# First columns of two matrices and second tokens loaded first; layer a's last step with rows in front of scores; the last rows and router pieces placed among later expert blocks

## The chip, the cores and the metric

The kernel runs on one core of one Trainium2 chip. The core has five engines with queues of their own: TensorE (PE in the profile, its weight loads PEld), VectorE (DVE), ScalarE (ACT), GpSimd (POOL) and SyncE (SP), which here only issues DMAs. Engines wait for each other by semaphores. The metric is the device time of one execution in microseconds (us); lower is better.

## The reference

Eight batches of 512 tokens with 256 features, in float32, go through four layers, each with a residual:

```
x = x + attention_a(layernorm(x))   # 16 heads of 64, causal, a linear bias by distance, out-projection with bias
x = x + experts(layernorm(x))       # RMS norm, router, the best 2 of 8 experts per token, gated two-layer MLP
x = x + attention_b(layernorm(x))   # 8 heads of 128, causal, rotary positions
x = x + experts(layernorm(x))       # the same expert weights again
```

Attention is `softmax(q k^T + bias) v` for each head, and the expert layer is

```
vals, idx = top_k(flat @ gate_w.T + gate_b, 2);  wts = softmax(vals)
t1 = einsum('td,efd->tef', flat, mlp1_w) + mlp1_b
y  = einsum('tei,edi->ted', swiglu(t1), mlp2_w) + mlp2_b
out = sum(y[idx] * wts)
```

## The kernel before

The four layers are one long program. `layer` emits an attention layer, `Experts.run` the expert layer behind it.

**Order of the instructions.** Only TensorE is scheduled by hand (`manual_schedule`, L120): it executes in the order in which the code emits. The other engines are ordered by the framework's planner, which takes the ready instruction that was emitted earliest; a DMA issue on SP counts as one. Once built, each engine's order is fixed, and an instruction that waits holds up all behind it on its engine.

**Attention.** A layer has 64 steps (b, g): batch b, head group g, two heads of layer a or one of layer b. A step (`step`, L503) of layer a emits the scores of the current group in three PSUM banks, then turns the probabilities of the group before (`turn`, 20 transposes in all), between them the q and k projections of the next group and the "extra" pieces due at this place, and at the end `average` of the group before. `scores` sends each bank through DVE (bias and row maximum, L407) and ACT (exponential with sums, L417); the rows are then divided by their sums, the longest by DVE and the other three by POOL (L434), and for the very last group of a layer all by DVE. `turn` copies the turned rows out by ACT, one bank of six by DVE (L457 to L459).

**Extras.** `layer` files every other piece under a key (b, g, k): the values, the out-projection, the norm of the next batch ((b, 5, 1), then applied and turned at (b, 6)), the router of the previous batch. What would fall behind the last batch is returned as a list: the last turns, the last average, two out-projections of the last half, and six router pieces of the last batch.

**Experts.** Tokens are gathered by expert into 71 blocks of 128 rows. `run` (L1049) is a pipeline over iterations n: it gathers block n + 4, turns the activations of block n - 5, turns the rows of block n (`turn_rows`), does the first matrix of block n - 2 (`first`) and the second matrix of block n - 6 (`second`), then the pieces that `aside` holds for n. `flush` (L1195) places the returned list and the second stage's six sorting pieces at iteration numbers.

`turn_rows` transposes a gathered row block and lets ACT copy it back: for the blocks below AHEAD (L86) in place, into the gather tile `g` (tag "qk", four blocks a tile, two tiles), for the others into the tile `turned`, which has the tag "O" (one buffer) and so takes the place of the attention's output O once the last out-projection has read it.

**Start.** `layers` issues on SP the tokens of batch 0 (two of four pieces on ACT's queue), then whole matrices: wq and wk (1 MB each, two rows of 4 KB per partition), alibi, the output bias, wv, wo, the router's constants, and the expert weights `we` in 16 pieces (6 MB together), then sin (L152 to L175). Batch b + 1's tokens are fetched by a piece at (b, 1, 1), into one of three "x" buffers (L1220). `fold_norm` lets POOL multiply the expert weights by the norm's weights (L243, 16 times).

Of the kernel before, what the change touches and what calls it, by code (L numbers as in the profile page):

```python
# [37 lines left out]
F32 = mybir.dt.float32  # L38
# [8 lines left out]
P = 128  # L47
NB, T, D = 8, 512, 256
NT = T // P
NC = D // P  # L50
INNER = 1024
# [31 lines left out]
LEAD = 4  # L83
ROWS = 4
DEPTH = 6
AHEAD = 3  # L86

W_COLS = NC * 2 * FI + FI // P * D
B_COLS = 2 * FI + D
# [4 lines left out]
def layers(  # L94
# [24 lines left out]
    nc = tc.nc  # L119
# [4 lines left out]
    wpool = ctx.enter_context(tc.tile_pool(name="wpool", bufs=1))  # L124
# [7 lines left out]
    def load(pool, shape, src, name, tag=None):  # L132
        t = pool.tile(shape, F32, tag=tag or name, name=name)
        nc.sync.dma_start(out=t, in_=src)
        return t

    def by_rows(w):
        return w.rearrange("(c p) n -> p c n", p=P)

    def by_tokens(x):  # L140
        return x.rearrange("(t p) d -> p t d", p=P)

    def load_x(src, name):
        return load(xpool, [P, NT, D], by_tokens(src), name, "x")

    X = {0: xpool.tile([P, NT, D], F32, tag="x", name="x0")}
    for t in range(NT):
        (nc.sync, nc.scalar)[t % 2].dma_start(
            out=X[0][:, t, :], in_=x_in[0][t * P : (t + 1) * P, :]
        )  # L150
    mask_sb = cos_sb = None
    wq = load(wpool, [P, NC, INNER], by_rows(a_qkv[:, 0:INNER]), "wq_a", "wq")  # L152
    wk = load(wpool, [P, NC, INNER], by_rows(a_qkv[:, INNER : 2 * INNER]), "wk_a", "wk")
    alibi_sb = load(const, [P, T], alibi, "alibi", "bias")
    bout_sb = load(const, [P, D], a_bout.partition_broadcast(P), "bout", "cos")
    wv = load(wpool, [P, NC, INNER], by_rows(a_qkv[:, 2 * INNER : 3 * INNER]), "wv_a", "wv")
    wo = load(wpool, [P, INNER // P, D], by_rows(a_out), "wo_a", "wo")
# [1 line left out]
    gatew_sb = load(const, [P, NC, NE], by_rows(gatew), "gatew")  # L159
    gateb_sb = load(const, [P, NE], gateb.partition_broadcast(P), "gateb")  # L160
    rank_sb = load(const, [P, NT, NE], rank, "rank")
    we_sb = const.tile([P, NE * W_COLS], F32, tag="we", name="we")
    be_sb = const.tile([P, NE * B_COLS], F32, tag="be", name="be")
    for e in range(NE):
# [3 lines left out]
            out=we_sb[:, o:mid].rearrange("p (c f) -> p c f", c=NC),  # L168
            in_=w1[:, e, :].rearrange("(c p) f -> p c f", p=P),
        )  # L170
        nc.sync.dma_start(
            out=we_sb[:, mid : o + W_COLS].rearrange("p (c d) -> p c d", c=FI // P),
            in_=w2[:, e, :].rearrange("(c p) d -> p c d", p=P),
# [106 lines left out]
    class Attention:  # L280
# [155 lines left out]
        def turn(self, b, g, i, n):  # L436

            key = f"{self.kind}_{b}_{g}_{i}"
            S = self.S[b, g][i][0]
            if n == 0:  # L440
                self.PT[b, g, i] = work.tile([P, PACKED], F32, tag="PT", name=f"PT_{key}")
            bank = P_BANKS[n]
            base = P_OFF[bank[0]]
            tp = ps.tile([P, T], F32, tag="ps", bufs=8, name=f"tp_{key}_{n}")
            width = 0
            for jt in bank:
                for it in range(jt, NT):
                    o = P_OFF[jt] - base + (it - jt) * P
                    nc.tensor.transpose(  # L449
                        tp[:, o : o + P],  # L450
                        S[:, S_OFF[it] + jt * P : S_OFF[it] + (jt + 1) * P],
                        ident,
                    )
                    width += P
            pt = self.PT[b, g, i][:, base : base + width]
            if n == 0 and i == 1:
                nc.vector.tensor_copy(pt, tp[:, 0:width])  # L457
            else:
                nc.scalar.copy(pt, tp[:, 0:width])  # L459
# [43 lines left out]
        def step(self, last, cur, after, extra):  # L503

            there = set(self.qk)

            def scores(n):
                if cur:
                    self.scores(*cur, n)

            def turn(i, *banks):
                if last:
                    for n in banks:
                        self.turn(*last, i, n)

            def project(j):
                if after and after not in there:
                    self.project(*after, j)

            if self.kind == "a":  # L520
                scores(0)
                scores(1)
                scores(2)
                turn(0, 0, 1, 2)
                project(0)
                extra(1)
                turn(1, 0, 1, 2)
                project(1)
                extra(2)
            else:  # L530
                scores(0)
                project(0)
                turn(0, 0)
                scores(1)
                project(1)
                turn(0, 1, 2)
                scores(2)
                extra(1)
                extra(2)
            if last:  # L540
                self.average(*last)


    class Experts:
# [401 lines left out]
        def turn_rows(self, i, j):  # L946
# [7 lines left out]

            if m < AHEAD:
                h = g
            else:
                if m == AHEAD:
                    self.turned = work.tile([P, HALF * T // D, D], F32, tag="O", bufs=1, name=f"hT_{self.kind}")
# [234 lines left out]

    def flush(left, exp):  # L1195

        turns = (0, 2, 2, 2, 3, 5, 8, 10, 12, 14)
        aside = {}
        for n, piece in zip(turns, left, strict=True):
            aside.setdefault(n, []).append(piece)  # L1200
        for n, piece in zip((16, 18, 20, 22, 25, 28), exp.sorting(1), strict=True):
            aside[n] = [piece]
        return aside

# [2 lines left out]
    def fetch_a(b):  # L1207
        X[b] = load_x(x_in[b], f"x{b}")
# [8 lines left out]
    att_a.project(0, 0, 0)  # L1217
    att_a.project(0, 0, 1)
    more = [((0, 3, 1), spread_biases), ((1, 0, 1), fold_norm)]
    more += [((b, 1, 1), lambda b=b: fetch_a(b + 1)) for b in range(NB - 1)]  # L1220
    aside = flush(layer(att_a, exp_a, more), exp_a)
    aside.setdefault(6, []).append(weights_b)
    aside[done] = [lambda: exp_a.fetch(0)]
# [13 lines left out]
    more = []  # L1237
    for b in range(NB - 1):
        more.append(((b, 0, 1), lambda b=b: exp_a.fetch(b + 1)))
        for t in range(NT):  # L1240
            more.append(((b, t, 1), lambda b=b, t=t: exp_a.collect(b + 1, (t,), "tmp", both_queues)))
            more.append(((b, t + 1, 1), lambda b=b, t=t: exp_a.add(b + 1, (t,))))
    aside = flush(layer(att_b, exp_b, more), exp_b)

    def store(b, tiles, engine):
# [11 lines left out]
    for k, (b, tt) in enumerate(halves):  # L1257
        n = done + 3 * k // 2
        tag = ("xT", "PT")[k % 2] if k not in (8, 9) else "qk"
# [5 lines left out]
    end = TOTAL + DEPTH  # L1265
# [76 lines left out]
```

## Time and profile before

| | us |
|---|---|
| median of 3 runs | 2254.11 (2252.29 to 2255.5) |
| the profiled execution | 2239.6 |
| its span, first to last instruction | 2237.8 |

The profile is of one execution, by the hardware's own records; times in the views are us from the start of the span. TensorE's granted clock is 0.993 of full speed over the span. The costliest places of TensorE, by its rows: the expert matrices L982 257.8 us, the transposes L449 of layer a 166.2 us, the scores of layer b 169.7 us and of layer a 155.5 us, the averages of layer a 156.0 us. A timeline row gives start, duration, engine, line, operation, tiles, count, and in brackets how long the engine was idle before it and what it waited for. Some matmuls are drawn as overlapping, since their ends are modelled; the distance of their starts is the better measure.

The three places that the change touches lie in the span as follows: the start at 0 to 60 us, the end of layer a and the first expert blocks at 915 to 1020, the end of layer b and its expert blocks at 1970 to 2070.

| window, us | PE busy | DVE | ACT | POOL | PE clock | GB/s by DMA |
|---|---|---|---|---|---|---|
| 0 to 20 | 15.91 | 8.58 | 5.93 | 7.60 | 1.00 | 291 |
| 20 to 40 | 18.02 | 8.79 | 9.46 | 18.32 | 1.00 | 357 |
| 40 to 60 | 17.82 | 12.00 | 10.70 | 7.36 | 0.91 | 45 |

### The profile page before, as it was taken

The page shows a single profiled execution, that of the slowest core. Times are in us where ns is not written, and L with a number is a line of the kernel's source. Part 1 is how long each engine was busy: PE and PEld are TensorE (multiplying, and loading weights), DVE is VectorE, ACT ScalarE, POOL GpSimd, SP SyncE. Part 2 cuts the span into 40 slices and gives each one's busy share as a digit, 9 for nine tenths or more (in the row PEclk, how much of TensorE's full clock was granted, in tenths as well). Part 3 has the DMA queues.
Part 4 walks back from the last instruction along what each step waited for, and adds up shares of the span by engine and source line. Part 5 has one row for each costly group of instructions (what it writes and reads, how often), then busy time and mean ns, then how long its engine had stood idle before and what let it go on. Part 6 is the DMA issues. An engine that isn't in the chain of part 4 may idle for free.

```text
span 2237.8 us, 33567 instructions
## 1 busy us (share of the span) xinstructions
PE 2190.3 (98%) x10513; PEld 1429.2 (64%) x10513; DVE 1586.9 (71%) x4817; ACT 961.6 (43%) x2784; POOL 967.1 (43%) x1337
## 2 busy tenths in 40 slices
PE   8999999999999999999999999999999999999995
PEld 5666666666666666656666666666666666665663
DVE  4566666666666687687787676777777678968768
ACT  4555555555555555323324334434444433333331
POOL 5443434243433333266654343333434343356662
PEclk9999999999999999999999999999999999999997
DMA  7100000000000000232220010100101010042237
GB/s 248 39 15 15 6 24 1 30 1 29 1 29 1 29 6 29 99 106 84 90 76 29 10 39 10 39 29 19 48 6 43 6 34 1 19 139 78 85 101 252
DMA packets 78382, 108.80 MB, mean 49 GB/s; under 512 B 9568, under 2 KB 64000, under 8 KB 78208
## 3 DMA queue, kind: packets, MB, share of 16 engines
q1 hardware_dynamic: 62656, 67.58, 9.4%
q0 software_dynamic: 13632, 37.24, 5.4%
q8 instruction: 87, 1.43, 0.3%
q10 hardware_dynamic: 1920, 1.84, 0.3%
q14 instruction: 87, 0.71, 0.1%
HBM read 67.02 MB, written 39.60 MB: 48 GB/s over the span
## 4 chain that ended last, share of the span: by engine, by line
PE 88%; DVE 7%; issue 2%; ACT 1%; POOL 1%; SPq 1%; DMA 1%; DVEq 0%; ACTq 0%; POOLq 0%
PE pp_b L337 10%; PE hp_f L982 9%; PE pp_a L337 9%; PE op_a L476 6%; PE sp_b L395 6%; PE sp_a L395 6%; PE tp_a L449 6%; PE op_b L476 6%; PE yp_a L494 5%; PE yp_b L494 5%; PE vp_a L318 4%; PE y_f L1021 4%; PE vp_b L318 4%; PE tp_b L449 3%; PE gtp_f L953 1%
## 5 line engine op out<-in xcount | busy, mean ns | idle before, releaser
L417 ACT ACTIVATE S_a<-S_a,nm_a 128x512 f32<-128x512 f32 (+3 forms) x512 | 280.1, 548 | 313.7 <-DVE nm_a L407 309.9
L350 POOL TENSOR_TENSOR qk_b<-qk_b,rot_b 128x512 f32<-128x512 f32 x128 | 163.0, 1274 | 453.1 <-DVE qk_b L349 427.7
L376 POOL TENSOR_SCALAR ali_a<-alibi 128x512 f32<-128x512 f32 x128 | 79.3, 620 | 454.9 <-DVE nm_a L407 443.1
L982 PE MATMUL hp_f<-we,hT_f 128*128 x544 | 257.8, 596 | 4.3 <-DVE u_f L993 2.9
L417 ACT ACTIVATE S_b<-S_b,nm_b 128x512 f32<-128x512 f32 (+3 forms) x256 | 142.9, 559 | 241.1 <-DVE nm_b L407 233.4
L407 DVE CUSTOM_DVE_ANT_0 S_a<-sp_a,ali_a 128x512 f32<-128x512 f32 (+3 forms) x512 | 215.9, 487 | 30.7 <-PE sp_a L395 30.7
L434 POOL TENSOR_SCALAR S_a<-S_a,sum_a 128x384 f32<-128x384 f32 x378 | 203.1, 554 | 34.6 <-DVE sum_a L428 25.0
L1033 POOL DMA_INDIRECT y_f<-y_f,row_f x142 | 143.4, 1010 | 114.1 <-DVE y_f L1032 59.2
L407 DVE CUSTOM_DVE_ANT_0 S_b<-sp_b,mask 128x512 f32<-128x512 f32 (+3 forms) x256 | 119.4, 485 | 77.1 <-PE sp_b L395 76.7
L395 PE MATMUL sp_b<-qk_b 128*128 128x512 f32 (+3 forms) x512 | 169.7, 434 | 2.6 <-POOL qk_b L350 2.5
L449 PE MATMUL tp_a<-ident,S_a 128*128 128x128 f32 x1280 | 166.2, 276 | 5.4 <-DVE O_a L484 3.3
L939 POOL DMA_INDIRECT g_f<-h_all_f,token_f x142 | 144.4, 1017 | 59.4 <-issue 39.6
L449 PEld LDWEIGHTS tp_a<-ident,S_a 128*128 128x128 f32 x1280 | 141.3, 142 | 36.8 <-issue 21.3
L994 ACT ACTIVATE u_f<-u_f 128x256 f32<-128x256 f32 x142 | 59.2, 417 | 238.0 <-DVE u_f L993 179.5
L476 PE MATMUL op_a<-PT_a,V_a 128*64 128x384 f32 (+3 forms) x1024 | 156.0, 442 | 3.3 <-ACT S_a L417 2.2
L1021 PEld LDWEIGHTS y_f<-we,aT_f 128*128 128x128 f32 x568 | 108.8, 193 | 77.1 <-issue 59.6
L395 PE MATMUL sp_a<-qk_a 64*128 64x512 f32 (+3 forms) x1024 | 155.5, 443 | 0.9 <-DVE qk_a L354 0.9
L1021 PE MATMUL y_f<-we,aT_f 128*128 x568 | 148.6, 385 | 3.8 <-ACT aT_f L1012 3.7
L459 ACT COPY PT_a<-tp_a 128x512 f32<-128x512 f32 (+1 forms) x320 | 139.1, 496 | 29.4 <-PE tp_a L449 27.6
L476 PE MATMUL op_b<-PT_b,V_b 128*128 128x512 f32 (+3 forms) x512 | 148.7, 433 | 0.0
L993 DVE TENSOR_TENSOR u_f<-hp_f,be 128x512 f32<-128x512 f32 x142 | 98.2, 691 | 59.5 <-PE hp_f L982 20.5
L982 PEld LDWEIGHTS hp_f<-we,hT_f 128*128 128x128 f32 x544 | 92.7, 190 | 73.1 <-issue 66.3
(205 smaller groups left out, 4454.8 us busy)
## 6 DMA issues: line engine op xcount, KB each, us to landing
h_all_f<-hn_f SPq DMA_DIRECT2D x64, 128.0 KB
xm_f<-x_mid_f SPq DMA_DIRECT2D x16, 512.0 KB
yg_f<-y_f SPq DMA_DIRECT2D x32, 256.0 KB
yg_f<-y_f SPq DMA_DIRECT2D x56, 128.0 KB
we<-w_dram SPq DMA_DIRECT2D x8, 512.0 KB
x_mid_f<-x SPq DMA_DIRECT2D x8, 512.0 KB
x_mid_f<-xm_f SPq DMA_DIRECT2D x8, 512.0 KB
x<-x_in_dram SPq DMA_DIRECT2D x7, 512.0 KB
```

Source lines behind the costliest of these rows:

```text
L318: nc.tensor.matmul(vp[:, k, :], lhsT=self.xT[b][:, c, t * P : (t + 1) * P], rhs=wv[:, c, q * 2 * P : (q + 1) * 2 * P], start=(c == 0), sto ...
L337: nc.tensor.matmul(pp, lhsT=w[:, c, g * P : (g + 1) * P], rhs=self.xT[b][:, c, :], start=(c == 0), stop=(c == NC - 1),)
L350: nc.gpsimd.tensor_tensor(qk[:, j, :], qk[:, j, :], rot, ALU.add)
L395: nc.tensor.matmul(sp[i][:, at[it] : at[it] + w], lhsT=qk[r, 0, it * P : (it + 1) * P], rhs=qk[r, 1, 0:w], start=True, stop=True,)
L407: nc.vector.tensor_tensor_reduce(out=s, in0=sp[i][:, at[it] : at[it] + w], in1=add[i][:, T - w : T], scale=scale, scalar=float(np.finfo(np ...
L417: nc.scalar.activation(s, s, AF.Exp, bias=nm[:, it : it + 1], scale=-1.0, accum_out=sums[:, it : it + 1],)
L434: eng.tensor_scalar(s, s, sums[:, it : it + 1], 1.0, ALU.mult, ALU.mult)
L449: nc.tensor.transpose(tp[:, o : o + P], S[:, S_OFF[it] + jt * P : S_OFF[it] + (jt + 1) * P], ident,)
L476: nc.tensor.matmul(op[i * cols : (i + 1) * cols, jt * P : T], lhsT=v[:, jt, c0 : c0 + cols], rhs=PT[i][:, P_OFF[jt] : P_OFF[jt] + T - jt * P],
L494: nc.tensor.matmul(yp[:, 0:D], lhsT=o[:, c, t * P : (t + 1) * P], rhs=wo[:, half * HALF + c, :], start=(c == 0), stop=(c == HALF - 1),)
L982: nc.tensor.matmul(hp, lhsT=h[:, c * P : (c + 1) * P], rhs=we_sb[:, bass.DynSlice(wat + c * 2 * FI, 2 * FI)], start=(c == 0), stop=(c == N ...
L1021: nc.tensor.matmul(yp, lhsT=aT[:, c * P : (c + 1) * P], rhs=we_sb[:, bass.DynSlice(wat + NC * 2 * FI + c * D, D)], start=(c == 0), stop=(c ...
```

## The change

The diff has four parts. At the start, wq and wk are each loaded in two pieces: the first 256 of 1024 columns of both, then alibi, then the other 768 columns of both. Batch 1's tokens are loaded in front of the expert weights instead of by the piece at (0, 1, 1). The last step of layer a emits the turns of the group before in front of the scores, without projections (there is no next group). `flush`, for both layers, puts the list's pieces two iterations later (the last, the count, three), and the sorting pieces one to two later; AHEAD goes from 3 to 5, so that five blocks of rows are kept in place and O's buffer is taken over later.

```diff
-AHEAD = 3
+AHEAD = 5
...
-    wq = load(wpool, [P, NC, INNER], by_rows(a_qkv[:, 0:INNER]), "wq_a", "wq")
-    wk = load(wpool, [P, NC, INNER], by_rows(a_qkv[:, INNER : 2 * INNER]), "wk_a", "wk")
+
+    wq, wk = (wpool.tile([P, NC, INNER], F32, tag=tag, name=f"{tag}_a") for tag in ("wq", "wk"))
+
+    def load_qk(first, end):
+        for k, w in enumerate((wq, wk)):
+            nc.sync.dma_start(
+                out=w[:, :, first:end],
+                in_=by_rows(a_qkv[:, k * INNER + first : k * INNER + end]),
+            )
+
+    load_qk(0, 2 * P)
     alibi_sb = load(const, [P, T], alibi, "alibi", "bias")
+    load_qk(2 * P, INNER)
...
     rank_sb = load(const, [P, NT, NE], rank, "rank")
+    X[1] = load_x(x_in[1], "x1")
...
-            if self.kind == "a":
+            if self.kind == "a" and not after:
+
+                turn(0, 0, 1, 2)
+                turn(1, 0, 1, 2)
+                for n in range(3):
+                    scores(n)
+                extra(1)
+                extra(2)
+            elif self.kind == "a":
...
-        turns = (0, 2, 2, 2, 3, 5, 8, 10, 12, 14)
+        turns = (2, 4, 4, 4, 5, 7, 10, 12, 14, 17)
...
-        for n, piece in zip((16, 18, 20, 22, 25, 28), exp.sorting(1), strict=True):
+        for n, piece in zip((18, 20, 22, 24, 26, 29), exp.sorting(1), strict=True):
...
-    more += [((b, 1, 1), lambda b=b: fetch_a(b + 1)) for b in range(NB - 1)]
+    more += [((b, 1, 1), lambda b=b: fetch_a(b + 1)) for b in range(1, NB - 1)]
```

## The prediction

> **What bounds the kernel.** I read the busy row and the chain of waits first, then TensorE's list of waits, then the timelines of the three places that the change touches.
>
> ```profile
> PE 2190.3 (98%) x10513; PEld 1429.2 (64%) x10513; DVE 1586.9 (71%) x4817; ACT 961.6 (43%) x2784; POOL 967.1 (43%) x1337
> PE 88%; DVE 7%; issue 2%; ACT 1%; POOL 1%; SPq 1%; DMA 1%; DVEq 0%; ACTq 0%; POOLq 0%
> ```
>
> TensorE (PE) is busy for 2190 of 2238 us and is 88% of the chain that ended last; most of VectorE's (DVE) 7% is the closing adds after the last matmul, at 2219 to 2234. The change removes no matmul, so it can win only PE's gaps before that tail, and what follows a gap. The gaps at its three places:
>
> ```profile
> PE tp_a L449 <- DVE O_a L484: 3.3, 2, 2.6
> PE op_a L476 <- ACT S_a L417: 2.2, 1, 2.2
> PE pp_a L337 <- DMA wk_a<-a_qkv_dram: 0.5, 1, 0.5
> PE tp_b L449 <- issue: 0.8, 1, 0.8
> PE yp_b L494 <- ACT O_b L486: 0.7, 1, 0.7
> ```
>
> Each line: waiter, releaser, us in total, times, longest. The first two cost more than they show, as the timelines (start, us, what, idle before) tell:
>
> ```profile
> 39.63 0.75 DVE L253 BATCH_NORM_STATS2 st_a<-x 128x6 f32<-128x256 f32 x2 [5.30 <-DMA x<-x_in_dram]
> 41.30 0.66 DVE L484 COPY O_a<-op_a 128x512 f32<-128x512 f32 x1
> ```
>
> ```profile
> 42.01 1.04 PE L449 MATMUL tp_a<-ident,S_a 128*128 128x128 f32 x6 [2.56 <-DVE O_a L484]
> 43.23 3.26 PE L337 MATMUL pp_a<-xT_a,wq_a 128*128 128x512 f32 x4 [0.17 <-DVE nm_a L407]
> 46.28 2.35 PE L318 MATMUL vp_a<-wv_a,xT_a 128*128 128x256 f32 x8
> 49.56 1.88 PE L337 MATMUL pp_a<-xT_a,wk_a 128*128 128x512 f32 x4
> ```
>
> DVE stands still 5.30 us for batch 1's tokens; the copy of O queues behind the statistics, and PE loses 2.56 us. Then four projection matmuls take 3.26 us instead of 1.88.
>
> ```profile
> 922.24 2.40 PE L449 MATMUL tp_a<-ident,S_a 128*128 128x128 f32 x20
> 926.88 1.07 PE L476 MATMUL op_a<-PT_a,V_a 128*64 128x512 f32 x2 [2.23 <-ACT S_a L417]
> 928.28 3.82 PE L476 MATMUL op_a<-PT_a,V_a 128*64 128x512 f32 x14 [0.34 <-issue]
> ```
>
> ```profile
> 928.00:932.00 4.00, 3.71 (x14) 1.67 (x14) 1.42 (x5) 0.86 (x2) 0.00 (x0) 0.59 0.13 37
> ```
>
> In layer a's last step the average waits while ScalarE (ACT) does the eight exponentials of step (7,7), which stand in front of its copies of the turned rows. In the last row (times by windows) the granted clock is 0.59.
>
> **The first gap's true price: a rule against a row.** The Trainium skill (TensorE: Matmul & The Clock Gate, Part 1) says that PE falls to half clock after an idle window of about 3.4 us, and its closing table allows gaps to about 3 us. By that rule, gaps of 2.56 and 2.23 us cost only themselves. The trace differs: in half-microsecond windows the clock is 0.50 from 44.0 to 46.5, and the pair of groups at 43.23 and 46.28 takes 1.38 + 0.46 = 1.8 us more than elsewhere (1.88 and 1.89); the 14 matmuls at 928.28 take 3.82 against about 2.05, 1.75 more. Yet a 2.23 us gap at 1886 leaves the clock at 1.00. So a gap of this size may double its price; here both did. By the rule the two waits are worth 2.7 + 2.6 us, by the rows 4.5 and 4.3; I take the rows.
>
> **Part 1, first columns first.** The k projection starts at 11.69, behind wk's load; q's ran from 9.20, when its weights' load had waited for xT too. The q and k columns needed first are 0.25 MB each, together half of wq, which had landed whole at 9.2. So they are there by then, and k can follow q at once, at 9.20 + 4 x 0.43 = 10.9: **0.8 us** earlier to the first scores. The columns behind (g = 2) are needed only at 28.9; wv is not late, since its bytes in front are the same. SyncE's queue (SP) gets two more issues, about 0.45 us each by its rows; at 7.21 to 13.4 it is held[...] anyway (gatew's issue takes 6.15), so between 0 and 0.9 us for what is behind. Here a rule speaks against the change: the skill (DMA: Bandwidth & Descriptors, section Bandwidth) wants transfers of 1 MiB and more, and its fit of 2.0 us plus bytes at 436 GB/s would make two extra pieces, run alone, an estimated 4 us dearer. The row: at 20 to 40 us pieces of 256 and 512 KB from this same queue move 357 GB/s, since they overlap. I charge nothing.
>
> **Part 2, batch 1's tokens in front of the expert weights.** They land where the first expert weights land now (20.85; equal bytes in front) plus up to 0.9: about 21.5, instead of 39.6. The 5.30 us stall at 34.3 goes: 2.56 + 0.17 + 1.8 = **4.5 us**. What is late next:
> - The 0.5 MB delays each expert weight by 0.5 / 0.36 = 1.4 us. GpSimd (POOL) scales those weights (16 x 0.69 us) in the gaps of its normalising:
>
> ```profile
> 25.75 0.69 POOL L243 TENSOR_SCALAR we<-we,normw 128x512 f32<-128x512 f32 x1
> 26.42 2.76 POOL L434 TENSOR_SCALAR S_a<-S_a,sum_a 128x384 f32<-128x384 f32 x6
> ```
>
> PE's transposes wait for the second row (27.41, idle 0.99). If POOL keeps this order, they start 1.4 us later, and a gap of 0.99 + 0.8 + 1.4 = 3.2 us would bring the half clock, 1.7 more: -3.1 in all. If fewer scalings stand in front, up to +0.8 stays.
> - All engines but PE are ordered by the framework's planner. It placed the statistics 5.3 us too early. If it does so again, after the first group's score reductions (end 19.1, then a gap of 1.4 for ACT), DVE stalls until 21.5, plus 2 us of statistics; the k copy at 22.37 then ends near 24.8, scores of group 1 start at 25.2 instead of 23.99, and the transposes at about 27.8: -0.4, since the wait for POOL swallows the rest.
>
> Between +0.8 and -3.1 I take -0.6, near the second bullet. Start: 4.5 - 0.6 = **3.9 us** (1.4 to 5.3).
>
> **Part 3, last step of layer a, pieces two blocks later.** Both orders have done the same work when iteration 4's matmuls end (block 2's first layer), now at 949.93. New order from 919.88: 20 transposes 2.36, to 922.2 (their rows, POOL's last S at 914.8, are ready; ACT is free to copy); scores 2.36, to 924.6; average 2.31, to 926.9, no wait, its copies being done near 923; three row turns 0.66, to 927.6. Then the **new wait**: block 0's matmul needs ACT's copy of its row, and ACT's exponentials (921.89 to 926.26) now run 2.36 later, to 928.6; copy 0.37 and the hand-over: 929.05, PE idle 1.5. Block 0 1.72, to 930.8. The last turns: DVE's normalised rows, now ready at 927.6 and 929.4, come at 929.9 and 931.8, in time; 20 transposes, to 933.1. Blocks 1 and 2 with their turns 2 x 1.94, average 2.31, projection 7.1: 946.4. Gain **3.5 us**. Bounds: the copy slips between exponentials (4.8); the copy is planned still later and the half clock returns (0.5).
>
> AHEAD = 5 keeps five rows in place, because the O buffer is freed only at iteration 4; then block 3 reads the first gather tile until about 948.4, and gather 8, which refills it, stands on POOL until then. Behind it POOL has the last batch's norm chain (now 947.46 to 952.5, no earlier in the new order) and further gathers. Row 8 is turned near 954.6; a gather at 949 lands well before. If POOL runs the whole norm chain first, it is some 1.2 us late: that is inside the bound. The sorting pieces move along and end at iteration 29 instead of 28; the second stage's first gather is at 37.
>
> **Part 4, the same delays in layer b** (its step order is unchanged). Average ends at 1976.34; the third gather leaves POOL at 1975.88, and its data burst ends near 1977.3, so row 2 costs some 0.6 us of idle; block 0 to 1979.4, last turns 1.10 (ready at 1977.8), blocks 1 and 2 3.9, average 2.16, projection 7.0 with 0.1 for ACT's copy (now 0.69 behind a table load): 1993.7 against 1994.91. **1.0 us**, bounds 0 and 1.5 (the two idles).
>
> **Sum.** 3.9 + 3.5 + 1.0 = 8.4 us. The profiled execution took 2239.6 (span 2237.8 and 1.8 around it) and would take 2231.2. The median shown is 2254.1, 14.5 above the profiled one; the same loss off it gives **2245.7**.
>
> **Rivals.**
> 1. *The start gives all back* (0.17): POOL keeps its order, the gap of 3.2 us and the half clock come, and the statistics stall DVE as well: 4.5 - 4.5 = 0, leaving 4.5: 2249.6. For it: POOL is 18.3 of 20 us busy from 20 to 40. Against: it has to be misplanned twice.
> 2. *Planning noise takes the ends* (0.13): ACT's row copies are put late in both layers, layer a gains 0.5, b nothing; with 3.9: 2249.7. For: DVE and ACT show such misorders (PE waits 1.0 at 966). Against: ACT is idle 8.4 us before 946.
> 3. *Slower* (0.20): the planner puts batch 1's statistics in front of DVE's **first k copy** (now 13.71). It decides there: DVE then stands until the tokens land, at 21.5, or near 25 if SP's queue is held for the small pieces as it is for gatew; with 2 us of statistics and the copy, the first scores start at 24.8 to 28.3 instead of 14.55: -10.2 to -13.7, half clock -1.7; the old stall's 4.5 and POOL's two waits, 1.2, come back: -6.2 to -9.7 for the start, and with the 4.5 of parts 3 and 4 a loss of 1.7 to 5.2: 2255.8 to 2259.3, say 2258.5. For: the planner expected these tokens 5 us too early. Against: at an equal error it expects them near 16, when that copy is past.
>
> Forecast: 0.50.
>
> **Range and chances.** The bounds add to 1.9 and 11.3; with the spread of runs, 1.6 either way, 2241 to 2254; I reach half a us further at both ends; rival 3 lies above and is left out. What can be told from no change is 0.2%, 4.5 us. Faster: 0.50 x 0.95, and half of rivals 1 and 2: 0.62. Slower: half of rival 3, 0.10; same: the rest, 0.28.
>
> **What would show it.** Right: no DMA wait before the statistics of batch 1, no half clock near 44 or 930; k's projection at 10.9; iteration 4 of layer a's experts done near 949.93 - 3.9 - 3.5 = 942.5. Wrong: a DMA wait on DVE before 20, POOL's first S later than 27, or PE idle over 2 us ahead of block 0. A norm chain ahead of gather 8, with PE waiting at row 8, would break part 3.

## The result, and the profile after

The changed kernel is slower by about a quarter of a per cent: median 2257.20 us of 20 runs (2252.84 to 2261.01) against 2250.92 (2243.05 to 2255.50) for 20 runs of the kernel before beside it, ratio 1.0027 with a 95% interval of 1.0019 to 1.0035. The forecast was 2245.7, which is 8.4 us under the 2254.1 that it counted from, with a range of 2241 to 2254; the change moved the time 6.3 us the other way. The profiled execution took 2257.87 us, span 2256.1, mean granted clock 0.990.

One caution first. The profiled execution of the kernel before, 2239.6 us, lies 11.3 us under the median of its 20 runs and under the fastest of them; that of the changed kernel lies at its median. The two traces stand 18.3 us apart where the medians stand 6.3; so what only these two traces show is not yet a loss of the change. The record does not say that they are of one chip; profiles of both kernels from one chip are used below.

The busy row and the chain's row of the page after:

```profile
PE 2195.6 (97%) x10513; PEld 1431.4 (63%) x10513; DVE 1587.7 (70%) x4817; ACT 960.7 (43%) x2784; POOL 959.9 (43%) x1337
PE 87%; DVE 8%; issue 2%; ACT 1%; DMA 1%; POOL 1%; DVEq 0%; SPq 0%; another core or an unknown queue 0%; POOLq 0%; ACTq 0%
```

TensorE still bounds it. Its list of waits (waiter, releaser: us in total, times, longest; hp_f and y_f are an expert block's first and second matrix, u_f and aT_f what VectorE and ScalarE make between them):

```profile
PE hp_f L1001 <- DVE u_f L1012: 7.7, 7, 2.2
PE y_f L1040 <- ACT aT_f L1031: 5.3, 5, 2.3
PE xtp_a L286 <- DVE xn_a L273: 4.3, 1, 4.3
PE gtp_f L972 <- DMA g_f<-h_all_f,token_f: 4.0, 3, 1.6
...
PE inv_f L900 <- DVE col_f L885: 1.7, 2, 0.9
```

Of the two waits that the prediction set out to remove, op_a for S_a is gone, and tp_a for O_a is down from 3.3 us in two waits to one of 0.7, the one that is not at the start. Two waits are new, gathered rows (gtp_f) and the sorting's tables (inv_f), and that of the first transposes of all (xtp_a) has grown from 0.3 us to 4.3.

**The start.** TensorE's timeline from 5 to 22 us:

```profile
10.09 2.23 PE L286 MATMUL xtp_a<-ident,xn_a 128*128 128x128 f32 x8 [4.28 <-DVE xn_a L273]
12.90 3.78 PE L348 MATMUL pp_a<-xT_a,wq_a 128*128 128x512 f32 x4 [0.57 <-DVE xT_a L317]
16.47 2.74 PE L348 MATMUL pp_a<-xT_a,wk_a 128*128 128x512 f32 x4
20.09 2.21 PE L406 MATMUL sp_a<-qk_a 64*128 64x512 f32 x14 [0.88 <-DVE qk_a L365]
```

and GpSimd's, in the same stretch:

```profile
5.37 0.20 POOL L267 TENSOR_SCALAR rs_a<-mv_a 128x4 f32<-128x4 f32 x1 [3.18 <-DVE mv_a L265]
7.45 0.61 POOL L387 TENSOR_SCALAR ali_a<-alibi 128x512 f32<-128x512 f32 x1 [1.88 <-DMA alibi<-alibi_dram]
8.14 1.04 POOL L268 TENSOR_TENSOR rs_a<-rs_a,mhalf 128x4 f32<-128x4 f32 x1
```

Alibi is now loaded behind 0.5 MB of weights instead of 2 MB, and the planner puts its scaling **between the two instructions of the first norm's root** (a scaling at L267 and a power at L268). GpSimd stands 1.88 us for alibi's DMA, the power ends near 9.2 instead of 6.45, VectorE's first normalised rows and TensorE's first transposes come 3 us late, and behind TensorE's gap of 4.28 us the projections run at half clock: 3.78 us for four matmuls instead of 1.95. The first scores come at 20.09 instead of 14.55. Batch 1's statistics then find their tokens there (VectorE's timeline, no wait in brackets):

```profile
22.45 0.75 DVE L264 BATCH_NORM_STATS2 st_a<-x 128x6 f32<-128x256 f32 x2
```

so the stall of 5.30 us, the gap at 42 and its half clock are gone, as forecast, and the two nearly cancel: in these two traces the scores of step (0,3) start at 53.9 instead of 55.4.

**The end of layer a.** Windows (PE, PEld, DVE, ACT, POOL busy with counts, clock, DMA share, GB/s) and TensorE's timeline:

```profile
0.00:20.00 20.00, 12.83 (x40) 7.84 (x40) 5.97 (x22) 2.46 (x3) 7.99 (x23) 0.74 0.92 304
40.00:60.00 20.00, 20.00 (x116) 12.89 (x115) 10.98 (x41) 12.05 (x39) 10.54 (x20) 1.00 0.15 46
928.00:932.00 4.00, 4.00 (x27) 3.12 (x26) 3.72 (x11) 2.90 (x5) 0.33 (x1) 1.00 0.19 58
```

```profile
922.71 2.37 PE L487 MATMUL op_a<-PT_a,V_a 128*64 128x512 f32 x16
925.01 0.87 PE L972 MATMUL gtp_f<-ident,g_f 128*128 128x128 f32 x6
927.13 1.98 PE L1001 MATMUL hp_f<-we,g_f 128*128 x4 [1.24 <-ACT g_f L980]
...
954.60 0.41 PE L972 MATMUL gtp_f<-ident,g_f 128*128 128x128 f32 x2 [1.61 <-DMA g_f<-h_all_f,token_f]
```

The average no longer waits, the clock from 928 to 932 is 1.00 instead of 0.59, and block 0 waits 1.24 us (forecast 1.5). Then row 8 waits 1.61 us for its gather. GpSimd's timeline says why:

```profile
945.82 0.20 POOL L267 TENSOR_SCALAR rs_f<-mv_f 128x4 f32<-128x4 f32 x1 [17.49 <-DVE mv_f L265]
...
950.89 0.31 POOL L618 TENSOR_TENSOR rs_f<-rs_f,rs_f 128x4 f32<-128x4 f32 x1
951.61 1.08 POOL L958 DMA_INDIRECT g_f<-h_all_f,token_f  x1 [0.41 <-issue]
```

The norm chain of the last batch runs first, gather 8 leaves at 951.61 and its rows can be turned 3.0 us later. In the kernel before (its GpSimd, then its TensorE) gather 8 also stood behind this chain, but row 8 was turned 5.2 us after it:

```profile
947.46 0.20 POOL L256 TENSOR_SCALAR rs_f<-mv_f 128x4 f32<-128x4 f32 x1 [19.53 <-DVE mv_f L254]
...
953.10 1.08 POOL L939 DMA_INDIRECT g_f<-h_all_f,token_f  x1 [0.58 <-PE gtp_f L953]
...
958.35 0.38 PE L953 MATMUL gtp_f<-ident,g_f 128*128 128x128 f32 x2
```

The change moved the chain 1.6 us forward and row 8's due time 5.4 (without its wait it would be 953.0).

### The profile page after: what moved, and what is told of

Read it like the earlier page. It is cut to its first block, busy times and chain, and to the rows that moved or that the text cites. A ratio compares the mean times of both kernels' runs of the same rounds, so it can differ in the third digit from the quotient of the medians.

```text
span 2256.1 us, 33549 instructions
## 1 busy us (share of the span) xinstructions
PE 2195.6 (97%) x10513; PEld 1431.4 (63%) x10513; DVE 1587.7 (70%) x4817; ACT 960.7 (43%) x2784; POOL 959.9 (43%) x1337
## 4 chain that ended last, share of the span: by engine, by line
PE 87%; DVE 8%; issue 2%; ACT 1%; DMA 1%; POOL 1%; DVEq 0%; SPq 0%; another core or an unknown queue 0%; POOLq 0%; ACTq 0%
PE pp_b L348 9%; PE pp_a L348 9%; PE hp_f L1001 8%; PE sp_a L406 6%; PE op_a L487 6%; PE tp_a L460 6%; PE sp_b L406 6%; PE op_b L487 5%; PE yp_a L505 5%; PE yp_b L505 5%; PE vp_a L329 5%; PE vp_b L329 4%; PE y_f L1040 4%; PE tp_b L460 3%; PE gtp_f L972 1%
## 5 line engine op out<-in xcount | busy, mean ns | idle before, releaser
L487 PE MATMUL op_a<-PT_a,V_a 128*64 128x256 f32 (+3 forms) x1024 | 153.5, 439 | 0.7 <-DVE PT_a L468 0.7
```

The costliest lines, as they stand in the source:

```text
L487: nc.tensor.matmul(op[i * cols : (i + 1) * cols, jt * P : T], lhsT=v[:, jt, c0 : c0 + cols], rhs=PT[i][:, P_OFF[jt] : P_OFF[jt] + T - jt * P],
```

## The experiments

My theory was that the new places of the pieces lose the time (theory 1); against it stood that any edit makes the planner order the engines anew, at a price of chance (theory 2), and that the start's order is what costs (theory 3). Ratios are to the kernel before, run beside each set. The record numbers the chip of every set but the result's: 3, 11, 0, 4, and 11 again. On chips 3, 11 and 4 the kernel before takes nearly the same time (2227.7 to 2229.4 us; "the three alike chips" below), on chip 0 2241.9, in the result 2250.9. To put a ratio of one set beside that of another is to compare chips too.

| kernel | ratio, 95% interval | chip | median of before, us |
|---|---|---|---|
| start_only | 0.9997 (0.9989 to 1.0005) | 3 | 2229.35 |
| last_only | 0.9994 (0.9986 to 1.0003) | 3 | 2229.35 |
| flush_only | 1.0032 (1.0020 to 1.0045) | 3 | 2229.35 |
| last_flush | 1.0023 (1.0013 to 1.0033) | 3 | 2229.35 |
| after_again | 1.0008 (1.0002 to 1.0015) | 11 | 2228.27 |
| even_sort | 1.0012 (1.0004 to 1.0020) | 11 | 2228.27 |
| free_rows | 0.9996 (0.9988 to 1.0004) | 11 | 2228.27 |
| both_fixes | 0.9995 (0.9987 to 1.0003) | 0 | 2241.94 |
| start_al | 0.9995 (0.9987 to 1.0003) | 0 | 2241.94 |
| x1_only | 0.9989 (0.9981 to 0.9998) | 0 | 2241.94 |
| fixed_all | 0.9986 (0.9979 to 0.9993) | 0 | 2241.94 |
| after_3rd | 1.0011 (1.0002 to 1.0019) | 4 | 2227.72 |
| after_rows | 0.9986 (0.9980 to 0.9993) | 4 | 2227.72 |
| norm_kept | 0.9977 (0.9969 to 0.9986) | 4 | 2227.72 |
| best | 0.9964 (0.9951 to 0.9978) | 4 | 2227.72 |
| free_rows_2 | 0.9993 (0.9984 to 1.0001) | 11 | 2228.27 |
| both_fixes_2 | 0.9987 (0.9980 to 0.9994) | 11 | 2228.27 |

### One part at a time

start_only has the diff's edits of the loads alone, last_only its new branch in `step`, flush_only AHEAD, `turns` and the sorting's places, last_flush the last two together.

> Only the two changes at the start (column pieces with alibi between them, batch 1's tokens early). Theory 1 (the loss comes from the new places of the flush pieces): the start keeps the 1.9 us that it had gained by step (7,6) in the changed kernel's trace, and both expert stages keep their old length, so about 2249 us, ratio 0.999. Theory 2 (any edit makes the framework's planner order VectorE, ScalarE and GpSimd anew, and a new order costs what it happens to cost): the expert stages lengthen here too, by several us, with no edit in them; ratio 1.002 to 1.005. In the first 20 us both expect GpSimd's scaling of alibi between the root-mean-square sum and its power, and TensorE's first scores near 20.

> Only the new order in the last step of layer a; pieces and AHEAD as before. Theory 1: the wait of the average for the turned rows (2.23 us) and the half clock behind it (1.8 us) go, one wait for the turned row in front of block 0 comes (1.5 us): some 2.5 to 4 us gained, about 2247.5 us, ratio 0.9985; expert stages as before. Theory 2: several us lost in the expert stages, ratio over 1.001.

> Only the later places of the pieces, the closer places of the sorting and AHEAD 5; the step order and the start as before. Theory 1: this holds the loss: both expert stages lose TensorE time to waits for VectorE's u_f and ScalarE's turned rows, 12 and 10 us by the changed kernel's trace against the trace of before, some 10 us in all by the medians (which stand only 6 apart with a gain of 5.5 from the other parts): about 2261 us, ratio 1.004 to 1.006. Theory 2: no more than start_only or last_only. If the late gather (8) alone were to blame, two waits of 1.6 us would be all: 2254, ratio 1.0015.

> The whole change without the start. Theory 1: as flush_only less the 3.65 us that the last step gained in the changed kernel's trace: about 2258 us, ratio 1.003 to 1.004. A third theory (the start's replanned order is what the later stages pay for): ratio at or below 0.999. Theory 2: no order between this and flush_only is foreseen.

The later pieces hold the loss: 0.3% by themselves, less than the 0.4 to 0.6% expected and without the waits for u_f, while start and last step alone can't be told from no change. In start_only and last_only the expert stages keep their length to 0.3 us between one another, so re-planning as such (theory 2) costs nothing there. last_only gains little because its transposes, moved to the front with no blocks between, wait 2.64 us at 928 for the rows that VectorE scales, and the half clock follows: the new order needs the later pieces. TensorE's timeline of last_flush shows what these cost:

```profile
957.12 0.41 PE L961 MATMUL gtp_f<-ident,g_f 128*128 128x128 f32 x2 [1.59 <-DMA g_f<-h_all_f,token_f]
...
1017.39 0.28 PE L889 MATMUL inv_f<-col_f,row_f 128*128 128x60 bf16 x4 [0.36 <-DVE col_f L874]
1019.07 0.27 PE L889 MATMUL inv_f<-col_f,row_f 128*128 128x60 bf16 x4 [1.40 <-DVE col_f L874]
...
2001.06 0.41 PE L961 MATMUL gtp_f<-ident,g_f 128*128 128x128 f32 x2 [1.56 <-DMA g_f<-h_all_f,token_f]
...
2062.70 0.27 PE L889 MATMUL inv_f<-col_f,row_f 128*128 128x60 bf16 x4 [1.40 <-DVE col_f L874]
```

Row 8 waits in **both** layers, and so does the first inversion of the second stage's sorting (inv_f, matmuls on the tables col_f), now two iterations behind the piece in front of it instead of three.

### The two waits taken away

even_sort is last_flush with the old distances, two iterations later; free_rows is last_flush with row 3's turned copy elsewhere:

```
-        turns = (2, 4, 4, 4, 5, 7, 10, 12, 14, 17)
+        turns = (2, 4, 4, 4, 5, 7, 10, 12, 14, 16)
...
-        for n, piece in zip((18, 20, 22, 24, 26, 29), exp.sorting(1), strict=True):
+        for n, piece in zip((18, 20, 22, 24, 27, 30), exp.sorting(1), strict=True):
```

```
-            if m < AHEAD:
+            if m == 3:
+                h = work.tile([P, D], F32, tag="tmp", bufs=3, name=f"early_{self.kind}")
+            elif m < AHEAD:
                 h = g
```

> last_flush with the last router piece at 16 in place of 17 and the sorting pieces at 18, 20, 22, 24, 27, 30, so with all the distances that they have in the kernel before. Theory 1a (the crowded sorting pieces cost): both waits for VectorE's col_f (1.8 us in layer a, 1.4 in layer b) go, some 3 us: ratio 1.0009 to 1.0011 in place of 1.0023. Theory 1b (the late gather alone): no change, 1.0022 or more, with both waits for gathered rows still there.

> last_flush with the turned row 3 copied to a buffer of its own instead of back into the first gather tile, so that this tile comes free at iteration 4, as in the kernel before, and gather 8 need not wait for block 3. Theory 1b: the waits of 1.6 us at row 8 in both layers go, and the half clock that followed in some runs: 3 to 5 us, ratio 1.0001 to 1.001. Theory 1a: at most these 3 us, and the waits for col_f stay. If what made gather 8 late is GpSimd's norm chain and not the tile, the waits stay and the ratio is 1.0023.

> The kernel before, unchanged, for a second profile beside those of the parts. Theory 1 expects the waits for gathered rows and for the tables of the sorting to be absent here, as in last_only, and the expert stages to differ from last_only's by under 1 us outside the last step. If TensorE's waits for VectorE's u_f (2.9 us in the first profile of before, none in last_only) come back, the chip and not the kernel makes them or not.

> The changed kernel, unchanged. The parts measured alone add to 1.0023 (last step and pieces) - 0.0003 (start) = 1.0020. Theory 4 (start and pieces together make a worse order than each alone: TensorE waited 7.7 us for u_f in the changed kernel's trace and not at all in last_flush): about 1.0027 to 1.003 again, with waits for u_f. Otherwise 1.002, and no waits for u_f.

The two waits are two causes. even_sort has no wait for col_f left; its ratio lies 0.0011 under last_flush's, as expected, but it ran on another chip and the intervals overlap. free_rows lies 0.0027 under last_flush with intervals that don't, and is better than the 1.0001 to 1.001 expected. In it GpSimd issues gathers 8 to 11 at 937.0 to 940.9, before the norm chain (946.95), since block 3 no longer holds their tile:

```profile
937.04 0.94 POOL L947 DMA_INDIRECT g_f<-h_all_f,token_f  x1 [7.58 <-ACT g_f L971]
```

Of TensorE's waits those for gathered rows fall from 3.9 us (three, the longest 1.6) to one of 1.1, while the sorting's stay:

```profile
PE inv_f L889 <- DVE col_f L874: 3.2, 3, 1.4
...
PE gtp_f L961 <- DMA g_f<-h_all_f,token_f: 1.1, 1, 1.1
```

after_again shows no wait for u_f (none either in last_flush, 0.2 us in before_again), so start and pieces together do not by themselves make the 7.7 us of the first trace: theory 4 fell. Nor do the parts quite add: 1.0008 and (below) 1.0011 against 1.0020. How the same TensorE work shifts from before_again to two profiles of the changed kernel, after_again on the same chip and after_3rd on an alike one (after minus before, us):

| point | after_again | after_3rd |
|---|---|---|
| scores of step (0,3) | +0.7 | +1.2 |
| scores of step (7,4) | +0.4 | +0.9 |
| layer a, block 3's first matrix | -2.8 | -2.3 |
| block 6's (row 8 just turned) | -0.7 | -0.3 |
| block 18's, 24's, 25's (inversion before it), 28's | -0.9, -2.1, 0.0, 0.0 | -0.5, -1.7, +0.4, +0.4 |
| layer b, block 0's | -0.8 | -0.4 |
| block 3's | +0.3 | +0.8 |
| block 6's | +2.4 | +2.9 |
| block 18's, 24's, 25's, 28's | +4.2, +3.4, +5.5, +5.5 | +3.0, +2.1, +4.2, +4.3 |
| end | +5.0 | +3.8 |

(By the medians the change costs 1.7 and 2.4 us on these chips, so 3.3 and 1.3 us of the ends are luck of the executions; before_again's was 2.9 us under the median.) Between blocks 24 and 25 the sorting loses 2.1 us each time, but 0.8 to 1.2 of them are gained before, since the pieces between blocks 18 and 24 now stand behind them: over the whole sorting, block 18 to 28, it is 0.9 us in layer a and 1.3 in layer b.

Both cures together, first on chip 0, then beside free_rows on one chip:

> The last step and the pieces with both cures: row 3 in a buffer of its own, and the router's last piece and the sorting at the old distances. If the two losses are separate and add: 1.0023 - 0.0011 - 0.0027 = 0.9985, about 3.3 us faster than before, with no wait for gathered rows of 1.6 us at row 8 and none for col_f. If one of the two took in the other, 0.9996 as with the buffer alone.

> free_rows once more: 0.9996 if its first ratio holds; waits for col_f of 1.4 us twice still there.

> both_fixes on the same chip as free_rows_2. If the closer sorting costs its two or three waits of 1.4 us and what follows (2 us each by the traces): 0.0011 to 0.0018 below free_rows_2, about 0.998 to 0.9985. If the even distances only move the wait to other places: within 0.0005 of free_rows_2.

both_fixes_2 lies 0.0006 under free_rows_2, with intervals that overlap; both_fixes on chip 0 gave 0.9995, not the 0.9985 of a plain sum. The traces of the pair part over the sorting (block 18 to 28) by 1.5 us in layer a and 1.1 in layer b; a half clock behind a 2.17 us gap at 1878, in the one execution and not in the other, takes 1.8 back. So the closer sorting costs 1.3 us by this pair's ratios, 2.5 by even_sort's, 2.6 by the traces. That it makes the waits is shown; what it costs in all is not clear of noise.

### The start

start_al is start_only with alibi loaded behind all four column pieces; x1_only has the early tokens alone; norm_kept has no load moved, and one edit:

```
-            nc.vector.bn_stats(out=st[:, t, :], in_=X[b][:, t, :])
+            made = nc.vector.bn_stats(out=st[:, t, :], in_=X[b][:, t, :])
+            if (key, b) == ("a", 1):
+                tc.keep_in_program_order(made)
```

> start_only with alibi loaded after all four pieces of columns instead of between them. Theory 3 (alibi, landing early, is put by the planner in front of GpSimd's power for the first root mean square, and the start's gain is lost to that): the power runs at 5.5 again, TensorE's first transposes at 7, the first scores near 14 instead of 20.2, no half clock from 8 to 18, and step (0,3) starts 4 to 5 us before start_only's: ratio 0.9975 to 0.998. If the planner puts another thing in front, or if batch 1's statistics then stall VectorE earlier, no better than start_only's 0.9997.

> Only batch 1's tokens in front of the expert weights; columns and alibi loaded as before. If the early tokens by themselves were good and the columns' order was what lost it: the stall of 5 us before batch 1's statistics and TensorE's 2.56 us wait at 42 go, first scores at 14 to 16 as before, ratio 0.998. If the tokens' place is what disturbs the start (statistics in front of the first copies, GpSimd's scaling of weights late): 1.000 or more, with a DMA wait on VectorE before 25.

In start_al the theory is right about alibi and wrong about the gain (0.9995). TensorE's timeline:

```profile
10.90 1.88 PE L348 MATMUL pp_a<-xT_a,wk_a 128*128 128x512 f32 x4
13.65 2.43 PE L406 MATMUL sp_a<-qk_a 64*128 64x512 f32 x16 [0.88 <-DVE qk_a L365]
...
27.04 3.95 PE L406 MATMUL sp_a<-qk_a 64*128 64x512 f32 x16 [3.87 <-DVE qk_a L365]
```

The k projection stands at 10.90, as the prediction had worked out, and the first scores at 13.65 (14.4 to 16.1 in the twelve profiles whose columns load as before). But now VectorE reaches batch 1's statistics before their tokens:

```profile
20.29 0.75 DVE L264 BATCH_NORM_STATS2 st_a<-x 128x6 f32<-128x256 f32 x2 [4.07 <-DMA x<-x_in_dram]
```

and the second scores wait 3.87 us, with half clock behind. x1_only shows the same stall (3.50 us; its ratio is 0.9989 all the same). The early load moved the stall; what makes it is the planner's place for the statistics. In the changed kernel alibi's delay had merely hidden it.

> before with one edit: the statistics of batch 1 stay where the program issues them, in step (0,5), and no load is moved. If the stall comes from their early place alone: VectorE's wait of 5 us at 34 and TensorE's 2.56 us at 42 go, with the half clock that follows in some runs: 2.6 to 4.5 us, ratio 0.998 to 0.9988. If what follows the statistics (GpSimd's root, the turned rows, the first projections of batch 1) comes late instead, 1.000 or more.

norm_kept came in at 0.9977, 4.6 us by the medians (3.1 to 6.9 by the interval). Its statistics run in step (0,5), at 84.58, and TensorE's turns at 38 to 40 are in one piece, with no wait:

```profile
38.39 1.66 PE L451 MATMUL tp_a<-ident,S_a 128*128 128x128 f32 x10
39.88 1.88 PE L339 MATMUL pp_a<-xT_a,wq_a 128*128 128x512 f32 x4
```

The scores of step (0,3) show all starts side by side: they begin at 53.4 to 56.1 us in ten profiles with the start of before, at 53.7 to 54.6 in five with the start of the change, at 52.9 and 53.1 with alibi behind the columns (start_al, fixed_all), and at 50.3 and 50.1 with the statistics kept in place (norm_kept, best).

### The whole

fixed_all is both_fixes with start_al's loads; after_rows is the whole change with row 3's own buffer; best is both_fixes with the columns (alibi behind them), tokens loaded as before and norm_kept's edit.

> both_fixes and start_al in one kernel: if the parts add, 0.9985 + 0.9978 - 1 = 0.996, some 8 us, which is what the prediction had expected of the change itself. If a new order of the whole costs again, the ratio is 0.998 or more.

> The changed kernel once more. If its loss belongs to the kernel alone: between 1.0008 and 1.0027 with intervals that overlap both, say 1.0017. If the chip decides how much the changed order of the expert stages loses, it follows the chip: near 1.001 with a time of before near 2229, near 1.0025 with one near 2250.

> The whole change with row 3 in a buffer of its own. The late gather was worth 0.0027 in last_flush; by that the ratio falls from 1.0008 to 1.0027 to between 0.998 and 1.000. If the planner's new order at the start and the sorting's closer places are the larger part, over 1.0005.

> The cures together: pieces and last step of both_fixes, first columns first with alibi behind them, tokens loaded where before loads them, statistics of batch 1 kept in the program's order. If the parts add: 0.9995 to 0.9985 for the pieces, 0.9985 for the start: 0.997 to 0.998, below fixed_all's 0.9986. If a new order of the whole takes it back, 0.9986 or more.

One buffer for one row turns the change from 1.0011 to 0.9986 on the same chip, 5.8 us by the medians. fixed_all, on chip 0, missed the 0.996 of a plain sum. best is the fastest, 0.9964, 7.1 us under the kernel before by the medians of its five runs and 8.0 by the ratio; at the three places two waits of over 1 us are left, for the rows that GpSimd scales in the start, and for block 0's turned row:

```profile
PE tp_a L461 <- POOL S_a L446: 1.7, 2, 1.4
...
PE hp_f L1004 <- ACT g_f L983: 1.2, 1, 1.2
```

after_3rd gave 1.0011 beside a before of 2227.7, so the expectation that the loss follows the chip held on one side. On the result's chip the changed kernel was measured in one set only, and none of the cures was measured there.

## Why the prediction was wrong, step by step

Two of the signs that the prediction had named for being wrong came: GpSimd's first S at 28.90, later than 27, and a norm chain ahead of gather 8 with TensorE waiting at row 8.

**Part 1 (0.8 us).** The columns did what was worked out, in start_al (10.90 against 10.9; first scores 0.9 earlier), and the smaller pieces cost nothing that shows: no matmul of the changed start waits for a load, and 343 GB/s moved from 20 to 40 us, 357 before. (The fit that spoke against them stands in the Trainium skill, DMA: Bandwidth & Descriptors, in the section on one DMA of the GpSimd path; these are SyncE's.) What failed is the account of what moves with them: alibi stands between the pieces and so lands earlier. The prediction counted SyncE's issues and left GpSimd's order untouched, where the planner then put alibi's scaling in front of the first power. That cost TensorE 3 us and a half clock.

**Part 2 (4.5 less 0.6).** The stall, the gap and the half clock went, worth what was said (norm_kept: 4.6 us). "I take -0.6" for what the planner does with the statistics was far too little. Where the start is not delayed, they stall VectorE for 3.5 to 4.1 us: this is the second bullet, whose size was put at 0.4, but they stand behind the second of the first group's score reductions and not behind the last, so that the other reductions and the k copy wait with them. Where the start is delayed, the delay costs as much. The start as changed gave 0.7 us by its ratio (0.9997), which can't be told from nothing, where 3.9 were expected. Rival 1's end was right, its way (GpSimd's scaled expert weights) was not; rival 3's (the first k copy) did not happen either, so that 2257.2 lies near its 2258.5 is chance. By itself a start that gives nothing would have left 2249.6, inside the range.

**Part 3, last step (3.5).** Right: from step (7,4) to block 3's matmuls after_again and after_3rd gain 3.15 and 3.14 us on before_again, the wait for block 0 is 1.24 against 1.5.

**Part 3, "a gather at 949 lands well before. If POOL runs the whole norm chain first, it is some 1.2 us late: that is inside the bound."** This is the step that failed, with the largest single loss. It set gather 8 in front of the norm chain; the chain runs first in the kernel before as well (947.46 to 952.5, gather 8 at 953.10). The wait is 1.6 us in place of none, and came twice, once in each layer, since Part 4 did not repeat the argument. By free_rows and after_rows the late gather is worth 0.0025 to 0.0027, some 6 us; the traces of last_flush and free_rows, and of after_3rd and after_rows, part by 2.1 us at each of the two rows, and what makes up the other 2 is not shown.

**"The sorting pieces move along."** They did not move along: their distances changed from 2, 3, 3 to 2, 2, 3, and the last router piece came a step closer to the first of them. Costed at nothing, they made two or three waits of up to 1.4 us, 1.3 to 2.6 us in all.

**Part 4 (1.0).** Row 2 waited 0.79 us as foreseen (0.6), and block 0 0.25 more; that takes the place of a wait of 0.8 for the last rows. The 0.69 us wait for O_b that was counted as gained is in the first profile of before and not in before_again. Measured in after_again: layer b's last average starts at 1966.35 in both kernels, block 3's first matrix 0.3 later than before, so 0.3 lost.

**The clock gate, rule against row.** Taking the row was right for both places in that one trace. In before_again the half clock follows the second gap and not the first (2.50 us). Which gaps it follows can be read from the traces; the last section has it.

**The range.** The upper bounds of the parts (5.3, 4.8, 1.5) add to 11.6, not to 11.3; the range is hardly touched by it.

**The sum.** 8.4 us were expected to be gained and 6.3 were lost, 14.7 apart. On chips 11 and 4 the change loses 1.7 and 2.4 us, 10.1 and 10.8 apart. By the experiments: the start 3.2 short, the late gathers 5.8, the sorting 1.3 to 2.6, Part 4 1.3; that makes 11.6 to 12.9, more than the miss but within what the intervals leave. After_3rd's trace against before_again's books: start +0.9, last step -3.1, late gathers +2.0 and +2.1, sorting +0.9 and +1.3, the last pieces of layer b +0.4, the rest -0.7, which makes +3.8. What the result's chip adds, some 4 us, is not explained by these parts.

## What to carry to other kernels

When a stage is pulled forward, list what the other engines do in the same stretch that is not pulled along, and check which of it falls due earlier than it is made: here a gather that had 2 us to spare behind a norm chain had none. When a load is moved, follow every load whose landing it shifts to the engine that consumes it, if a planner orders that engine. Pinning one instruction to the program's order took the stall away (norm_kept, 0.9977), where moving its data only moved the stall (x1_only, 0.9989; the intervals overlap). Distances between a producer and its consumer in a pipeline are part of the tuning: shift them all by the same amount.

## What the runs showed of the hardware

**Gaps and the half clock.** In 20 profiles, between 20 and 2190 us, I counted TensorE's gaps and whether a window of 2 us that begins from 2 us before the gap's end to 3 us behind it showed a clock under 0.97. Of gaps of 1.2 to 1.5 us 2 of 32 were followed by it, of 1.5 to 2.0 4 of 13, of 2.0 to 2.4 16 of 30, of 2.4 to 3.9 11 of 14. The same gap of 2.17 us before layer b's first scores is followed by it in 8 of the 20 executions and not in the others.

The clock records show what decides. Within an execution every stretch at half clock begins on a grid of steps of 3.413 us, whose place differs between executions, and in this range it lasts one step (once two), which costs 1.7 us. I put TensorE's idle time in each of the 12,659 full-clock steps beside the clock of the next one: after all 27 steps with 2.03 us idle or more the half clock came, after steps with 1.66 to 2.03 us 7 times of 15, after steps with less never. In the first trace of before the gap in front of 42.01 lay so that one step had 1.8 us idle; the gap of 2.23 us in front of 1888.44 was cut by a step's end into some 0.8 and 1.5 (length, PE, PEld, DVE, ACT, POOL, clock, DMA share, GB/s):

```profile
40.37:43.78 3.41, 1.60 (x8) 0.94 (x9) 3.41 (x17) 1.19 (x3) 2.40 (x4) 1.00 0.85 175
43.79:47.20 3.41, 3.41 (x7) 1.69 (x6) 2.01 (x12) 3.41 (x15) 1.49 (x3) 0.50 0.20 69
...
1883.57:1886.98 3.41, 2.64 (x10) 1.41 (x8) 3.32 (x11) 1.75 (x6) 0.64 (x1) 1.00 0.00 0
1886.98:1890.39 3.41, 1.95 (x5) 0.99 (x6) 2.71 (x8) 1.07 (x3) 3.27 (x4) 1.00 0.00 0
1890.40:1893.81 3.41, 3.41 (x15) 1.90 (x14) 3.28 (x9) 1.40 (x3) 0.25 (x1) 1.00 0.00 0
```

So a gap of some 2 us costs its length, or 1.7 us more, by where it falls on the grid; a gap under 1.66 us can only do it together with another in the same step. That is below the 3.4 us idle window and the 3 us allowance of the Trainium skill (TensorE: Matmul & The Clock Gate, Part 1 and its closing table), and it makes single profiles of one kernel differ by several us.

**Chips.** The same program took 2250.9, 2241.9 or 2228 us. On the result's chip VectorE and ScalarE stand still in the expert stages for several us where on chip 11, with the same order of instructions in the stretch compared (958 to 975), they don't. TensorE's waits for u_f go with it: 7.7 us in the result's profile and 2.9 in the first of before, 0.7 to 3.9 us in the four of chip 0, at most 0.2 us in those of the three alike chips. VectorE's timeline of the changed kernel on the result's chip:

```profile
961.77 0.29 DVE L1015 TENSOR_SCALAR u_f<-u_f 128x256 f32<-128x256 f32 x1
966.06 0.42 DVE L1051 TENSOR_TENSOR y_f<-y_f,be 128x256 f32<-128x256 f32 x1 [4.00 <-PE atp_f L1026]
```

and of after_again:

```profile
961.06 0.29 DVE L1015 TENSOR_SCALAR u_f<-u_f 128x256 f32<-128x256 f32 x1
961.27 0.41 DVE L1051 TENSOR_TENSOR y_f<-y_f,be 128x256 f32<-128x256 f32 x1
```

The matmuls that this instruction needs had started at 959.95 and 960.13, alike in both. The first profile of the kernel before has such stalls too, but fewer; what they are, and whether they are why the change lost 0.27% there and 0.1% on chips 11 and 4, stays open.
